# Fourier layer kernel on one Trainium2 core: the inverse row transform of even layers in 32x32 matmul tiles

## The chip, the cores and the metric

The kernel runs on one core of a Trainium2 chip. Time is the device time of one execution in microseconds (us). The kernel before was run 12 times: median 4052.37 us, from 4046.01 to 4058.81 us. One more execution was taken with the hardware profiler, and all views come from that one.

## The reference, cut to what matters

The input x has 8 images of 8 channels, 256 x 256, in float32. Two stages follow each other. The first adds to x a Fourier network of the group-normalised x; the second adds to the result the 3 x 3 maximum (dilation) of its own group-normalised copy.

```python
h = fc0(gn(x) and two coordinate planes)        # 4 groups of 10 channels, 1x1 convolution per group
for i in range(4):                              # the layers, l = 0 .. 3
    xf = rfft2(h); keep 24 row x 12 column frequencies; multiply by complex weights per group
    h1 = irfft2(that)
    h = h1 + conv1x1(h)
    if i < 3: h = swish(h)
h = fc2(swish(fc1(h)))                          # 10 -> 128 -> 2 channels per group
x = x + h
x = x + max3x3(gn(x))
```

The step that changes is the first half of the inverse transform: from the few kept frequencies to all 256 rows.

## The kernel before, in words

**Layout.** One image is held at a time in the tile `h` (128 partitions). The transforms are matmuls with constant tables. A layer `l` of an image `b` runs through these generators, each of which records its instructions and yields now and then:

- `spectrum_h` (or `spectrum_x` for l = 0): forward transform along rows, into the small tile B.
- `mix`: products with the complex weights on the vector engine (L360, L363); the result F is folded by 16 matmuls of 32 x 32 (L379, tile `p_f`) into the tile `fz` (10 channels x 4 groups x 32 frequencies). Each of the four partition quarters q of `p_f` holds three column frequencies; four copies (L395, recorded in the helper as L195 or L193) put them side by side into the first columns of `fz`. For l = 0 a small matmul (L386) and an add (L387) put the mean in.
- `rows_of`: the inverse transform along the rows. For even layers each of the 10 channels is one matmul with a 128 x 128 stationary block of `fz` (4 groups x 32 columns) and the table `rowg` of 264 columns (L405, tile `p_g`). `rowg` holds the same 32 frequencies four times, and the four quarters of `fz` add up in the contraction over 128 partitions. Odd layers use 16 narrower matmuls per channel (L410), with a 32-column output each. Each pair of channels takes one accumulator, which two copies (L195, tile `zt`) empty, and then the generator yields 0.7.
- `layer`: for each of 11 chunks, `burst` adds the inverse column transform (L483) to the 1x1 convolution (L480; L477 for l = 0) in the tile `p_z`; the scalar engine applies the activation (L489, L491).

**Work laid in between.** `head` is the fc1/fc2 part of the image before. It has 128 steps. A step has an fc1 part (L628, four matmuls with 32 rows and 128 output columns, two accumulators, tile `p_fc`; the scalar engine then applies SiLU, L630, once for each accumulator) and, at every second step, an fc2 part (L650, eight matmuls, one accumulator; the vector engine then adds it, L655 or L653). The main loop takes such steps at the yields of the layers, so that the order on the tensor, vector and scalar engines is fixed by the program. `dilate` (tile `m`, L697 to L714) runs in the same way at the yields of the bursts.

**Accumulators.** All of these use one pool in PSUM: `ps_z` hands out four slots in turn, whoever asks. A slot is written again only when what was in it has been read. So the k-th request waits for the readers of request k - 4.

```python
    def ps_z(name):
        return ps.tile([128, 2, 512], F32, tag="z", bufs=4, name=name)
```

Image 0 has no image before it, so its layers run without fc1 and fc2 steps; there the copies alternate between vector and scalar engine (`alone`).

Of the kernel before, what the change touches and what calls it, by code (L numbers as in the profile page):

```python
# [10 lines left out]
F32 = mybir.dt.float32  # L11
AF = mybir.ActivationFunctionType
ALU = mybir.AluOpType
# [5 lines left out]
HW = 256  # L19
NPIX = HW * HW  # L20
G = 4
WID = 10
# [10 lines left out]
NBLK = 3  # L33
NCH = 11
NQ = 4
CS = 2 * NCH
PIX = 2 * HW
DR = 2
# [6 lines left out]
def fno_dilate_kernel(ctx: ExitStack, tc: tile.TileContext, a: dict, out: bass.AP):  # L45
    nc = tc.nc
    mm = nc.tensor.matmul
# [46 lines left out]
    xe = load("xe", (128, 6, G, 5), nc.sync)  # L94
    wext = const.tile([128, G, WID, 5], F32, tag="c_wext", name="c_wext")
    nc.sync.dma_start(wext.rearrange("p g o j -> p (g o j)"), a["wext"].partition_broadcast(128))
    cz = load("cz", (32, 5, WID, G))
    fold = load("fold", (128, 3, 32))
    rowg = load("rowg", (128, NBLK, NQ, CS))
    binv = load("binv", (128, HW))  # L100
    eh_f = load("eh_f", (128, 3, NBLK, 32))
# [70 lines left out]
    for l in range(3):  # L172
# [4 lines left out]
    nc.vector.tensor_tensor(cz[0:1, 0], cz[0:1, 0], cv[0:1], ALU.add)  # L177
    nc.sync.dma_start(cz[25:26, 0], cv[1:2])
    nc.sync.dma_start(cz[0:1, 4], cv[2:3])
    nc.vector.tensor_tensor(  # L180
        wt, wt, io.rearrange("p (l g) -> p l g", l=4).unsqueeze(3).to_broadcast([128, 4, G, 32]), ALU.mult,
    )
# [170 lines left out]
    def mix(b, l, out_):  # L353

        s = [sb.tile([128, 3, G, 2, WID], F32, tag=f"S{i}", bufs=1, name=f"S{i}_{b}_{l}") for i in range(2)]
        bt, sw = out_["bt"], out_["sw"]
        for k in range(3):
            for k2 in range(2):
                pr = turned[:, 2, 1024 * k2 : 1024 * k2 + 800].rearrange("p (g m i) -> p g m i", g=G, i=WID)
                nc.vector.tensor_tensor(  # L360
                    pr, sw[k], bt[:, k2, k].unsqueeze(2).to_broadcast([128, G, 2 * WID, WID]), ALU.mult)
                yield 0.7
                nc.vector.tensor_reduce(  # L363
                    s[k2][:, k].rearrange("p g s o -> p (g s o)"),
                    pr.rearrange("p g m i -> p (g m) i"), AX.X, ALU.add,
                )
                if k == 0 and k2 == 1:
                    sw.append(load_sw(l, 2))
                yield 0.7
        f = sb.tile([128, 2, 3, G, WID], F32, tag="F", bufs=1, name=f"F_{b}_{l}")  # L370
        nc.vector.tensor_tensor(f[:, 0], s[0][:, :, :, 0, :], s[1][:, :, :, 1, :], ALU.subtract)
        nc.vector.tensor_tensor(f[:, 1], s[0][:, :, :, 1, :], s[1][:, :, :, 0, :], ALU.add)
        yield 0.5

        p = ps_a(f"p_f_{b}_{l}")
        for slot in range(2):
            for n, (table, part_of) in enumerate(((0, slot), (1 + slot, 1 - slot))):
                for q in range(4):
                    mm(p[part(q), 120 * slot : 120 * slot + 120], fold[part(q), table, :],  # L379
                       f[part(q), part_of].rearrange("p k g o -> p (k g o)"), start=n == 0, stop=n == 1)  # L380
        nc.vector.tensor_copy(fz[0:32, :, :, 24], cz[:, l])
        if l == 0:
            mr = out_["mr"]
            d = sb.tile([128, 1], F32, tag="d", name=f"dm_{b}")
            nc.vector.tensor_tensor(d, mr[:, 0:1], mr[:, 1:2], ALU.mult)
            mm(p[0:1, 240 : 240 + WID * G], d, wm.rearrange("p o g -> p (o g)"), start=True, stop=True)  # L386
            nc.vector.tensor_tensor(  # L387
                fz[0:1, :, :, 24], fz[0:1, :, :, 24],
                p[0:1, 240 : 240 + WID * G].rearrange("p (o g) -> p o g", o=WID), ALU.add)
        if l < 2:  # L390
            nc.vector.tensor_copy(fz[0:32, :, :, 25], cz[:, 4 if l == 0 else 3])
        for q in range(4):
            dst = fz[part(q), :, :, 6 * q : 6 * q + 6].rearrange("p o g k -> p k g o")
            src = p[part(q), :240].rearrange("p (k g o) -> p k g o", g=G, o=WID)
            copy(q, dst, src)  # L395
        yield 2.5

    def rows_of(b, l):

        zv = zt[:, :, :, : NBLK * WID].rearrange("p r f (n o) -> p o n r f", n=NBLK)  # L400
        for o in range(0, WID, 2):
            p = ps_z(f"p_g_{b}_{l}_{o}")
            for u in range(2):
                if l % 2 == 0:
                    mm(p[:, u, : NBLK * CS * NQ], fz[:, o + u].rearrange("p g k -> p (g k)"),  # L405
                       rowg.rearrange("p n j r -> p (n j r)"), start=True, stop=True)
                else:
                    for g in range(G):
                        for j in range(NQ):
                            mm(p[part(j), u, NBLK * CS * g : NBLK * CS * (g + 1)], fz[:, o + u, g, :],  # L410
                               rowg[:, :, j, :], start=True, stop=True)
            for u in range(2):
                src = p[:, u, : NBLK * CS * NQ]
                if l % 2 == 0:
                    dst = zv[:, o + u].rearrange("p n r f -> p n f r")
                    src = src.rearrange("p (n f r) -> p n f r", n=NBLK, r=CS)
                else:
                    dst = zv[:, o + u].rearrange("p n r f -> p f n r")
                    src = src.rearrange("p (f n r) -> p f n r", f=NQ, n=NBLK)
                copy(u, dst, src)  # L420
            yield 0.7


    def layer(b, l, out_, stored, side):
# [254 lines left out]
    def dilate(b, stats):  # L679
        d = {}  # L680
        yield from stats_end(stats, f"y{b}", d)
        mr = d["mr"]
        whole = y_rows[b % 2][:]
        o_rows = out[b].rearrange("c (p f) -> (c p) f", p=16)
        for r in range(0, 16, DR):
            nc.gpsimd.dma_start(
                yin[:, :, 1 : HW + 1],
                bass.AP(whole.tensor, whole.offset + r * HW, [[16 * HW, 128], [HW, DR + 2], [1, HW]]))
            yield
            yield  # L690

            if r == 0:
                nc.vector.tensor_scalar(yin[:, 0, :], yin[:, 0, :], edge[:, 0:1], None, ALU.min)
            if r == 16 - DR:
                nc.vector.tensor_scalar(yin[:, DR + 1, :], yin[:, DR + 1, :], edge[:, 1:2], None, ALU.min)
            m = sb.tile([128, DR + 2, HW], F32, tag="m", bufs=1, name=f"m_{b}_{r}")
            nc.vector.tensor_tensor(m, yin[:, :, 0:HW], yin[:, :, 1 : HW + 1], ALU.max)  # L697
            yield
            nc.vector.tensor_tensor(m, m, yin[:, :, 2 : HW + 2], ALU.max)
            yield  # L700
            o = sb.tile([128, DR, HW], F32, tag="o", bufs=1, name=f"o_{b}_{r}")
            nc.vector.tensor_tensor(o, m[:, 0:DR], m[:, 1 : DR + 1], ALU.max)
# [12 lines left out]
            yield  # L715
# [73 lines left out]
def _tables():  # L789
# [50 lines left out]
    for j, v in enumerate(planes):  # L840
# [9 lines left out]
    edge[:, 2], edge[:, 3] = np.where(top, PAD, -BIG), np.where(bottom, PAD, -BIG)  # L850
    tables = {
        "fw": fw, "fw8": fw8, "stack": np.tile(np.eye(32), (4, 1)), "eh0": eh0, "eh_f": eh_f.reshape(128, 3, NBLK, 32),
        "rowg": rowg.reshape(128, NBLK, NQ, CS),
        "fold": fold.reshape(128, 3, 32), "binv": binv.reshape(128, HW),
        "xe": xe.reshape(128, 6, G, 5), "grp": grp, "edge": edge,
    }
    return {k: np.ascontiguousarray(v, f32) for k, v in tables.items()}
# [66 lines left out]
```

## Time and profile before

| | |
|---|---|
| median of 12 runs | 4052.37 us |
| profiled execution, its own time | 4050.78 us |
| its span, from the first to the last instruction | 4049.0 us |
| TensorE (PE) busy | 3740.0 us, 92% |
| ScalarE (ACT) busy | 2853.5 us, 70% |
| VectorE (DVE) busy | 2538.3 us, 63% |
| mean granted TensorE clock | 0.976 |
| row matmuls of even layers (L405) | 93.2 us busy, 320 records of 160 matmuls |
| folding matmuls (L379) | 36.7 us busy, 1024 records of 512 matmuls |

A float32 matmul leaves two records in the profile, one for each of its passes. "Busy" is the union of the records of a group, so that matmuls that run at the same time count once. In the chain of waits each stretch of time is put down to the instruction that held up the end.

### The profile page before, as it was taken

The page shows a single profiled execution, that of the slowest core. Times are in us where ns is not written, and L with a number is a line of the kernel's source. Part 1 is how long each engine was busy: PE and PEld are TensorE (multiplying, and loading weights), DVE is VectorE, ACT ScalarE, POOL GpSimd, SP SyncE. Part 2 cuts the span into 40 slices and gives each one's busy share as a digit, 9 for nine tenths or more (in the row PEclk, how much of TensorE's full clock was granted, in tenths as well). Part 3 has the DMA queues.
Part 4 walks back from the last instruction along what each step waited for, and adds up shares of the span by engine and source line. Part 5 has one row for each costly group of instructions (what it writes and reads, how often), then busy time and mean ns, then how long its engine had stood idle before and what let it go on. Part 6 is the DMA issues. An engine that isn't in the chain of part 4 may idle for free.

```text
span 4049.0 us, 118640 instructions
## 1 busy us (share of the span) xinstructions
PE 3740.0 (92%) x53530; PEld 1465.7 (36%) x53530; DVE 2538.3 (63%) x3535; ACT 2853.5 (70%) x2991; POOL 117.3 (3%) x202
## 2 busy tenths in 40 slices
PE   5666999999999999999999999999999999999997
PEld 2333333333333333333333333333333433333222
DVE  6665656556766666765766666666676566673533
ACT  3334777777767777776777777777777777778886
POOL 1000000000000000000000000000000000000000
PEclk8887999999999999999999999999999999999999
DMA  3005111441215321252122611144211532215311
GB/s 84 14 14 187 51 34 42 135 127 57 60 49 176 97 63 58 79 179 63 56 66 89 198 44 52 54 134 151 58 59 49 171 101 64 60 49 192 96 53 46
DMA packets 113986, 345.05 MB, mean 85 GB/s; under 512 B 15769, under 2 KB 18393, under 8 KB 98057
## 3 DMA queue, kind: packets, MB, share of 16 engines
q1 hardware_dynamic: 95288, 276.33, 22.1%
q0 software_dynamic: 18192, 61.13, 4.7%
q8 instruction: 422, 6.91, 0.7%
q14 instruction: 84, 0.68, 0.1%
HBM read 213.40 MB, written 123.74 MB: 83 GB/s over the span
## 4 chain that ended last, share of the span: by engine, by line
PE 78%; DVE 11%; ACT 7%; issue 3%; DMA 1%; POOL 0%; DVEq 0%; POOLq 0%; SPq 0%; ACTq 0%
PE p_fc L650 22%; PE p_fc L628 20%; PE p_z L483 8%; PE p_z L480 7%; PE p_d L448 6%; ACT act L630 4%; PE p_u L462 3%; DVE turned L431 3%; PE p_z L477 2%; PE p_b L333 2%; PE p_g L405 2%; PE p_g L410 2%; ACT h L491 2%; DVE turned L324 2%; DVE turned L201 1%
## 5 line engine op out<-in xcount | busy, mean ns | idle before, releaser
L630 ACT ACTIVATE act<-p_fc 128x1024 f32<-128x1024 f32 x2048 | 1960.2, 1026 | 674.3 <-PE p_fc L628 670.0
L628 PE MATMUL p_fc<-hs,c_w 32*128 32x512 f32 x8192 | 1205.2, 631 | 14.7 <-DVE turned L195 8.5
L650 PE MATMUL p_fc<-act,c_w 128*32 128x512 f32 x8192 | 1001.4, 603 | 47.2 <-ACT act L630 36.0
L628 PEld LDWEIGHTS p_fc<-hs,c_w 32*128 32x128 f32 x8192 | 402.2, 183 | 697.7 <-ACT act L630 278.2
L489 ACT ACTIVATE h<-p_z 128x1024 f32<-128x1024 f32 x528 | 511.8, 1021 | 189.1 <-PE p_z L483 187.7
L431 DVE STREAM_TRANSPOSE turned<-h 128x1024 f32<-128x1024 f32 x528 | 622.9, 1219 | 21.4 <-ACT h L489 21.1
L655 DVE TENSOR_TENSOR y<-p_fc,y 128x512 f32<-128x512 f32 x392 | 270.6, 690 | 498.1 <-PE p_fc L650 496.9
L650 PEld LDWEIGHTS p_fc<-act,c_w 128*32 128x32 f32 x8192 | 227.8, 110 | 649.5 <-issue 348.9
L483 PE MATMUL p_z<-c_binv,zt 32*128 32x256 f32 x5632 | 411.1, 405 | 0.6 <-ACT zt L193 0.6
L480 PE MATMUL p_z<-h,c_wt 32*32 32x512 f32 x8448 | 370.4, 601 | 6.3 <-DVE y L655 2.8
L483 PEld LDWEIGHTS p_z<-c_binv,zt 32*128 32x128 f32 x5632 | 261.4, 186 | 304.5 <-issue 295.0
L448 PE MATMUL p_d<-turned,c_fw 32*32 32x480 f32 (+1 forms) x9216 | 309.5, 539 | 12.5 <-DVE turned L431 12.5
L195 DVE COPY zt<-p_g 128x264 f32<-128x264 f32 x300 | 162.3, 628 | 168.0 <-PE p_g L410 91.4
L491 ACT ACTIVATE h<-p_z,c_bias 128x1024 f32<-128x1024 f32 x176 | 186.6, 1111 | 37.8 <-PE p_z L483 37.5
L199 ACT ACTIVATE turned<-p_d 128x960 f32<-128x960 f32 x144 | 130.2, 904 | 95.5 <-PE p_d L448 95.5
L363 DVE TENSOR_REDUCE S<-turned 128x80 f32<-128x800 f32 x192 | 188.7, 983 | 4.7
L360 DVE TENSOR_TENSOR turned<-t,B 128x800 f32<-128x800 f32 x192 | 188.4, 981 | 1.8 <-DMA t<-in_spw 1.7
L448 PEld LDWEIGHTS p_d<-turned,c_fw 32*32 32x32 f32 x9216 | 121.3, 103 | 187.8 <-issue 150.2
L462 PE MATMUL p_u<-turned,c_stack 128*32 128x480 f32 (+1 forms) x1152 | 137.3, 546 | 42.9 <-DVE turned L201 42.9
L324 DVE STREAM_TRANSPOSE turned<-zt 128x960 f32<-128x960 f32 x96 | 175.5, 1853 | 0.6
L201 DVE COPY turned<-p_d 128x960 f32<-128x960 f32 x144 | 152.1, 1057 | 29.2 <-PE p_d L448 28.9
L480 PEld LDWEIGHTS p_z<-h,c_wt 32*32 32x32 f32 x8448 | 93.6, 103 | 210.6 <-ACT act L630 69.1
(169 smaller groups left out, 1969.5 us busy)
## 6 DMA issues: line engine op xcount, KB each, us to landing
stored<-h SPq DMA_DIRECT2D x88, 1024.0 KB
hs<-stored SPq DMA_DIRECT2D x352, 256.0 KB
t<-in_spw SPq DMA_DIRECT2D x96, 400.0 KB
yin<-y_rows POOLq DMA_DIRECT2D x56, 512.0 KB, 4.9
h<-in_xp SPq DMA_DIRECT2D x352, 48.0 KB
turned<-in_x SPq DMA_DIRECT2D x16, 1024.0 KB
y<-in_x SPq DMA_DIRECT2D x56, 256.0 KB
y_rows<-y POOLq DMA_DIRECT2D x56, 256.0 KB, 2.3
```

The costliest lines, as they stand in the source:

```text
L324: nc.vector.transpose(rows[:, 960 * g : 960 * (g + 1)].rearrange("p (i r) -> p i r", r=32), windows(g))
L431: nc.vector.transpose(dst[:, 2 * i : 2 * i + 2], h[:, c, 2 * i : 2 * i + 2].rearrange("p f (s x) -> p f s x", s=2))
L448: mm(pair[q // 2][part(v % 4), q % 2, : 240 * n], fw8[part(q), v, :], t[part(q), :, :, v, : NBLK * WID], start=v < 4, stop=v >= 4)
L462: mm(p[part(g), : 240 * n], stack, m, start=True, stop=True)
L480: mm(o, wt[part(q), l, g, :], h[part(q), c, f, :], start=True, stop=False)
L483: mm(pair[q // 2][:, q % 2, HW * s : HW * (s + 1)], zt[part(q), 2 * c + s].rearrange("p f o -> p (f o)"), binv[part(q), :], start=False, s ...
L489: nc.scalar.activation(dst, pair[i], AF.Silu)
L491: nc.scalar.activation(dst, pair[i], AF.Identity, bias=bias3)
L628: mm(pair[g // 2][:, g % 2, :], w1[part(g), blk, :], hs[k][part(g), :], start=True, stop=True)
L630: nc.scalar.activation(act[:, 2 * i : 2 * i + 2, :], pair[i], AF.Silu)
L650: mm(acc[part(g), :], w2[:, g, 15 - rb - i : 47 - rb - i], act[:, g, :], start=i == 0, stop=i == 1)
L655: nc.vector.tensor_tensor(y, sums, y, ALU.add)
```

## The change

Even layers: `rowg` is no longer summed over four partition quarters. The fold table is repeated four times along its columns, so that the fold of one quarter q writes its three column frequencies to all four partition quarters; `fz` then holds four full copies of the spectrum. The row matmuls take one copy each: four channels at once, channel u from partition quarter u, with a 32 x 32 stationary tile for each group. Ten matmuls become forty smaller ones, and the blocks are of 4, 4 and 2 channels in place of five pairs. The yields add up to the same 3.5.

The fold needs four accumulators of its own (two requests to the pool, `pair`, in place of one). Odd layers still contract over 128 partitions, and now meet four copies; so the table is divided by 4, and in even layers the copies from `p_f` and the constants `cz` are multiplied by 4. The tile `cz` is spread to four quarters by three DMAs at the start. For l = 0 the mean is put in by four matmuls and four adds. The dilation writes its maximum over `m`, and the tile `o` goes.

```diff
-    fold = load("fold", (128, 3, 32))
+    fold = load("fold", (128, 3, 128))
...
+    for l in (0, 2, 4):
+        nc.vector.tensor_scalar(cz[0:32, l], cz[0:32, l], 4.0, None, ALU.mult)
+    for q in range(1, 4):
+        nc.sync.dma_start(cz[part(q)], cz[0:32])
...
-        p = ps_a(f"p_f_{b}_{l}")
+        pair = [ps_z(f"p_f_{b}_{l}_{i}") for i in range(2)]
+        p = [pair[q // 2][:, q % 2, :] for q in range(4)]
         for slot in range(2):
             for n, (table, part_of) in enumerate(((0, slot), (1 + slot, 1 - slot))):
                 for q in range(4):
-                    mm(p[part(q), 120 * slot : 120 * slot + 120], fold[part(q), table, :],
+                    mm(p[q][:, 120 * slot : 120 * slot + 120], fold[part(q), table, :],
                        f[part(q), part_of].rearrange("p k g o -> p (k g o)"), start=n == 0, stop=n == 1)
...
-            mm(p[0:1, 240 : 240 + WID * G], d, wm.rearrange("p o g -> p (o g)"), start=True, stop=True)
-            nc.vector.tensor_tensor(
-                fz[0:1, :, :, 24], fz[0:1, :, :, 24],
-                p[0:1, 240 : 240 + WID * G].rearrange("p (o g) -> p o g", o=WID), ALU.add)
+            for q in range(4):
+                mm(p[0][32 * q : 32 * q + 1, 240 : 240 + WID * G], d, wm.rearrange("p o g -> p (o g)"),
+                   start=True, stop=True)
+            for q in range(4):
+                row = slice(32 * q, 32 * q + 1)
+                nc.vector.tensor_tensor(
+                    fz[row, :, :, 24], fz[row, :, :, 24],
+                    p[0][row, 240 : 240 + WID * G].rearrange("p (o g) -> p o g", o=WID), ALU.add)
...
         for q in range(4):
-            dst = fz[part(q), :, :, 6 * q : 6 * q + 6].rearrange("p o g k -> p k g o")
-            src = p[part(q), :240].rearrange("p (k g o) -> p k g o", g=G, o=WID)
-            copy(q, dst, src)
+            dst = fz[:, :, :, 6 * q : 6 * q + 6].rearrange("p o g k -> p k g o")
+            src = p[q][:, :240].rearrange("p (k g o) -> p k g o", g=G, o=WID)
+            if alone[0] and q % 2:
+                nc.scalar.activation(dst, src, AF.Identity, scale=factor)
+            else:
+                nc.vector.tensor_scalar(dst, src, factor, None, ALU.mult)
...
-        for o in range(0, WID, 2):
-            p = ps_z(f"p_g_{b}_{l}_{o}")
-            for u in range(2):
-                if l % 2 == 0:
-                    mm(p[:, u, : NBLK * CS * NQ], fz[:, o + u].rearrange("p g k -> p (g k)"),
-                       rowg.rearrange("p n j r -> p (n j r)"), start=True, stop=True)
...
+        rows = rowg.rearrange("p n j r -> p (n j r)")
+        size = 2 if l % 2 else 4
+        for o in range(0, WID, size):
+            n = min(size, WID - o)
+            p = [ps_z(f"p_g_{b}_{l}_{o}_{i}") for i in range((n + 1) // 2)]
+            for u in range(n):
+                for g in range(G):
+                    if l % 2 == 0:
+                        mm(p[u // 2][part(g), u % 2, : NBLK * CS * NQ], fz[part(u), o + u, g, :], rows[part(u)],
+                           start=True, stop=True)
+                        continue
...
-            yield 0.7
+            yield 0.35 * n
...
-            o = sb.tile([128, DR, HW], F32, tag="o", bufs=1, name=f"o_{b}_{r}")
-            nc.vector.tensor_tensor(o, m[:, 0:DR], m[:, 1 : DR + 1], ALU.max)
+            o = m[:, 0:DR]
+            nc.vector.tensor_tensor(o, o, m[:, 1 : DR + 1], ALU.max)
...
-        "rowg": rowg.reshape(128, NBLK, NQ, CS),
-        "fold": fold.reshape(128, 3, 32), "binv": binv.reshape(128, HW),
+        "rowg": rowg.reshape(128, NBLK, NQ, CS) / 4.0,
+        "fold": np.tile(fold.reshape(128, 3, 32), (1, 1, 4)), "binv": binv.reshape(128, HW),
```

More of the change, by code (lines that the diff above doesn't have):

```diff
@@ L96, in fno_dilate_kernel @@
     nc.sync.dma_start(wext.rearrange("p g o j -> p (g o j)"), a["wext"].partition_broadcast(128))
-    cz = load("cz", (32, 5, WID, G))
-    fold = load("fold", (128, 3, 32))
+    cz = const.tile([128, 5, WID, G], F32, tag="c_cz", name="c_cz")
+    nc.gpsimd.dma_start(cz[0:32], a["cz"])
+    fold = load("fold", (128, 3, 128))
     rowg = load("rowg", (128, NBLK, NQ, CS))
@@ L378, in mix @@
                 for q in range(4):
-                    mm(p[part(q), 120 * slot : 120 * slot + 120], fold[part(q), table, :],
+                    mm(p[q][:, 120 * slot : 120 * slot + 120], fold[part(q), table, :],
                        f[part(q), part_of].rearrange("p k g o -> p (k g o)"), start=n == 0, stop=n == 1)
-        nc.vector.tensor_copy(fz[0:32, :, :, 24], cz[:, l])
+        factor = 4.0 if l % 2 == 0 else 1.0
+        nc.vector.tensor_copy(fz[:, :, :, 24], cz[:, l])
         if l == 0:
@@ L384, in mix @@
             d = sb.tile([128, 1], F32, tag="d", name=f"dm_{b}")
-            nc.vector.tensor_tensor(d, mr[:, 0:1], mr[:, 1:2], ALU.mult)
-            mm(p[0:1, 240 : 240 + WID * G], d, wm.rearrange("p o g -> p (o g)"), start=True, stop=True)
-            nc.vector.tensor_tensor(
-                fz[0:1, :, :, 24], fz[0:1, :, :, 24],
-                p[0:1, 240 : 240 + WID * G].rearrange("p (o g) -> p o g", o=WID), ALU.add)
+            nc.vector.scalar_tensor_tensor(d, mr[:, 0:1], factor, mr[:, 1:2], ALU.mult, ALU.mult)
+            for q in range(4):
[6 more added lines that the diff above has]
+                    p[0][row, 240 : 240 + WID * G].rearrange("p (o g) -> p o g", o=WID), ALU.add)
         if l < 2:
-            nc.vector.tensor_copy(fz[0:32, :, :, 25], cz[:, 4 if l == 0 else 3])
+            nc.vector.tensor_copy(fz[:, :, :, 25], cz[:, 4 if l == 0 else 3])
         for q in range(4):
-            dst = fz[part(q), :, :, 6 * q : 6 * q + 6].rearrange("p o g k -> p k g o")
-            src = p[part(q), :240].rearrange("p (k g o) -> p k g o", g=G, o=WID)
-            copy(q, dst, src)
+            dst = fz[:, :, :, 6 * q : 6 * q + 6].rearrange("p o g k -> p k g o")
[4 more added lines that the diff above has]
+                nc.vector.tensor_scalar(dst, src, factor, None, ALU.mult)
         yield 2.5
@@ L400, in rows_of @@
         zv = zt[:, :, :, : NBLK * WID].rearrange("p r f (n o) -> p o n r f", n=NBLK)
-        for o in range(0, WID, 2):
-            p = ps_z(f"p_g_{b}_{l}_{o}")
-            for u in range(2):
-                if l % 2 == 0:
-                    mm(p[:, u, : NBLK * CS * NQ], fz[:, o + u].rearrange("p g k -> p (g k)"),
-                       rowg.rearrange("p n j r -> p (n j r)"), start=True, stop=True)
[L407 to L413, printed above, removed]
+        rows = rowg.rearrange("p n j r -> p (n j r)")
[9 more added lines that the diff above has]
+                        continue
+                    for j in range(NQ):
+                        mm(p[0][part(j), u, NBLK * CS * g : NBLK * CS * (g + 1)], fz[:, o + u, g, :],
+                           rowg[:, :, j, :], start=True, stop=True)
+            for u in range(n):
+                src = p[u // 2][:, u % 2, : NBLK * CS * NQ]
                 if l % 2 == 0:
```

## The prediction

> **What bounds the kernel now.** I read the page first: TensorE is busy 92%, and the chain of waits gives it 78% of the span. The row matmuls that change (L405) hold 2% of that chain, about 81 us; that is the most that can be won. Next I read the chain through one interleaved even layer (image 2, l = 2); columns are start, duration, engine and line, number of records.
>
> ```profile
> 1105.06 1.07 PE p_fc L628 x8
> ...
> 1106.16 1.02 PE p_f L379 x32
> 1107.18 1.25 PE p_fc L628 x8
> 1108.43 1.85 PE p_fc L650 x16
> 1110.29 1.07 PE p_fc L628 x8
> 1111.36 1.09 PE p_g L405 x4
> 1112.45 1.21 PE p_fc L628 x8
> 1113.65 1.09 PE p_g L405 x4
> ...
> 1117.67 1.98 PE p_g L405 x8
> 1119.65 1.23 PE p_fc L628 x8
> 1120.88 1.09 PE p_g L405 x4
> ...
> 1126.06 2.05 PE p_z L480 x32
> ```
>
> The reader is to see that TensorE never rests here and that the five pairs cost 1.09 + 1.09 + 1.98 + 1.09 = 5.25 us. But L628 takes 1.07 us after some neighbours and 1.21 to 1.25 after p_f and p_g: something else is nearly late. The timeline shows what (start, duration, engine, line, operation):
>
> ```profile
> 1104.99 1.14 PE L628 MATMUL p_fc<-hs,c_w 32*128 32x512 f32 x8
> 1106.23 1.94 ACT L630 ACTIVATE act<-p_fc 128x1024 f32<-128x1024 f32 x2 [0.39 <-PE p_fc L628]
> 1107.11 1.32 PE L628 MATMUL p_fc<-hs,c_w 32*128 32x512 f32 x8
> ```
>
> An fc1 part takes 1.07 us of TensorE, but ACT empties its two accumulators only 1.24 us after its start and for 1.94 us more (about 0.97 each). So a slot that the next fc1 must share with this one is free 2.26 us (first) and 3.23 us (second) after the fc1's start, 0.05 for the signal included. At 1107.11 the second half of fc1 needs the first of these and starts 0.19 us late. Four slots go round, and that distance is what the change touches. The chain of an odd layer (image 2, l = 1) shows the same in the fold:
>
> ```profile
> 982.64 1.03 ACT act L630
> 983.67 0.04 issue
> 983.72 1.02 PE p_f L379 x32
> 984.74 1.85 PE p_fc L650 x16
> 986.60 2.50 PE p_fc L628 x16
> ```
>
> Here the fold itself waits for a SiLU of the fc1 two before it. The profiled execution took 4050.78 us (span 4049.0 and 1.8 around it), 1.6 below the median, so my sum starts from 4050.8.
>
> **Row matmuls of even layers.** Removed are 10 matmuls, 5.25 us per layer. Added are blocks of sixteen, sixteen and eight 32x32 matmuls of 264 columns. The nearest row is L480 in the same chain where nothing is late (1007.50, 32 records of 32x32 with 512 columns, 1.11 us): same tiles, same spread over accumulators. One record of 264 columns streams in 0.22 us (records of one L405 pair start 0.22 apart), one of 512 in 0.43. Two passes shorter by 0.21 each give 0.68 us per block; bounds are 0.44 (two passes and nothing else) and 1.11 (L480's own price). Three blocks: 2.0 us. Taken alone, 3.2 us less per layer.
>
> [...]
>
> **Slots of the row blocks.** A block of four channels asks for two slots in a row where a pair asked for one. The order of the built programs on TensorE in l = 2 is: before, fold, fc1, fc2, fc1, pair, fc1, pair, fc2, fc1, two pairs, fc1, pair, fc2, fc1, fc1, burst; after, fold, fc1, fc2, fc1, block, fc1, fc2, fc1, block, fc1, half block, fc2, fc1, fc1, burst. Wherever fc1, block, fc1 stand together, the block takes two of the four slots, and the second fc1 needs exactly both slots of the first. It can't finish its start before 3.23 us after the first one's start, and the next instruction follows 1.07 us after its second half begins (987.97 to 989.03 in the trace). So fc1, block, fc1 costs 4.30 us whether the block takes 0.4 or 1.1; before, fc1, pair, fc1 cost 1.07 + 1.09 + 1.21 = 3.37.
>
> **The fold takes two slots, too.** It moves from one slot to two, in all 32 layers. In even layers fc1, fold, fc1 also becomes 4.30 us, against 3.37 (1104.99 to 1108.36). In odd layers the order is fc1, fc1, fold, fc2, fc1, fc1: the fold's second accumulator is the first fc1's second slot, released one SiLU later (+0.97), with TensorE standing at the fold and fc2 and two fc1 queued behind it.
>
> The fold's own matmuls go from 32 to 128 output columns. Its eight rounds (16 matmuls, two passes, four quarters at once) start 0.10 us apart now. The row for loads of 128 columns one after another is L250: sixteen in 1.73 us, 0.108 each. So eight rounds take 0.87 us, against about 0.95 from start to next start now; no gain or loss that I count. Upper bound: the load's whole duration (L628, 183 ns mean), 1.47 us, +0.6.
>
> **The walk, l = 2** (from the fc1 at 1104.99 as zero). Before: fc2 at 3.37, fc1 at 5.23, and the burst at 21.07, its second half, which waits for the last-but-one fc1's SiLU, at 21.98, the column matmuls at 23.06. After: fc2 at 4.30, +1.86 fc1 at 6.16, block 7.23 to 7.91, fc1's second half at 6.16 + 3.23 = 9.39, fc2 10.46, fc1 12.32, block 13.39, fc1's second half 15.55, half block 16.62 (0.65), fc2 17.27, fc1 19.13, burst's second half at 19.13 + 3.23 = 22.36, column matmuls 23.44. Net +0.4 us: the 3.2 us is spent in three waits. At the block's upper bound +0.8, with a wait less 0 or below: -0.6.
>
> **The walk, l = 0** (six of them, images 2 to 7). The same from the fc1 at 1337.38, with one more price: four adds in place of one (L387, 0.21 each) delay the copies out of the first fold slot until about 4.6, where fc2 wants it at 4.3. Then fc1 6.46, second half 9.69, two fc2 (3.57) from 10.76, fc1 14.33, block, second half 17.56, half block 18.63, fc1 19.26, fc1, burst's second half 22.49 and column matmuls 23.57, against 1360.29 - 1337.38 = 22.91 now. Net +0.65, bounds -0.5 and +1.1.
>
> **The walk, odd layers** (14 of them, images 1 to 7). The second part of the fold starts at 984.66 and not at 983.72; it ends near 985.5, fc2 follows at 985.55 in place of 984.67. The copies out of the fold end 0.9 later and the vector add of fc2 behind them too; the second fc1 needs that add, as now. Net +0.87, bounds 0.6 and 1.5 (slow loads). What follows is TensorE alone up to the burst, so it stays late.
>
> **What is hidden or small.** The copies into `fz` go to 128 partitions, but the width along the partition is the same: an operation on 128 x 40 takes 219 ns (L340) and on 1 x 40 213 (L387). The ten copies out of `p_g` are the same ten (0.63 each). In l = 2 and l = 0 they end before the slots are wanted. The dilation's new maximum over `m` must wait until the output DMA has read `m`; that DMA is issued at 1274.07 and `m` is next written at 1287.64, 13.6 us of cover; a full exposure would be some us for each of 56. At the start three multiplications (0.18 each) and three DMAs on SP stand ahead of seven x-plane loads, which the first burst needs only at 69 us: +0.4. Image 0 has no fc1; there copies set the pace, and smaller blocks start them earlier: about -0.8 for each of its two even layers, +0.6 for the adds. Image 1, l = 0 has no fc1 before its fold: -1.5.
>
> **The sum.** 14 x 0.87 = 12.2; 7 x 0.4 = 2.8; 6 x 0.65 = 3.9; image 1, l = 0 -1.5; image 0 and the start -0.6. Together +16.8: 4050.8 + 16.8 = 4067.6 us. About 0.2% (8 us) is what a measurement of this kernel can tell from no change; this is twice that.
>
> **Rivals.** (1) Faster: the slots don't bind and the row matmuls' 3.2 us arrive on TensorE's chain, 13 x 3.2 + 2.1 = 44 us, 4007 us. For it speaks that the chain is nearly all PE; against it, that both programs' orders make fc1 wait for its predecessor's SiLU. It decides if SiLU's release comes earlier than 2.26 and 3.23 us, below about 1.1 and 2.1. (2) No change: the odd layers pay 12 us, but the even ones come out near their lower bounds (7 x -0.6 + 6 x -0.5 = -7) and with -2.1 the rest is +3, 4054. (3) Slower still: loads of the fold are not hidden (+0.6 in 14 odd layers, 8 us) and blocks cost L480's 1.11 (+0.4 in 13), together 4081.
>
> **How the numbers follow.** My walk 0.62, at 4058 to 4078 (even layers 0.4 us either way, odd ones at 0.7 to 1.0). No change 0.14, faster 0.13, slower still 0.11. Range 4050 to 4080: it leaves out the fast rival and about half of (3). Faster by over 0.2%: 0.13, within 0.14, slower 0.62 + 0.11 = 0.73.
>
> **What would show it.** Right: L405's successor holds about 32 us busy in place of 93; yet fc1 (L628's successor) behind p_f and p_g lasts 2 us in the chain in place of 1.2; ACT takes a larger share of the chain; in odd layers the fold is split by a wait of nearly 1 us. Wrong: fc1 behind a block starting at once, or blocks over 1.2 us, or output DMAs showing up as what `m` waits for.

## The result, and the profile after

The changed kernel takes 4063.65 us (median of 11 runs, 4058.85 to 4068.35); the kernel before, run beside it, 4050.63 us (45 runs, 4040.5 to 4059.42). The ratio is 1.0032, 95% interval 1.0024 to 1.0040: 13 us slower. The profiled execution took 4065.15 us (span 4063.4), 14.4 more than that of before.

The page of the kernel after, its first part and the chain's shares by engine:

```profile
PE 3728.3 (92%) x54538; PEld 1438.7 (35%) x54538; DVE 2528.4 (62%) x3562; ACT 2851.9 (70%) x2991; POOL 117.0 (3%) x202
...
PE 76%; DVE 11%; ACT 8%; issue 4%; DMA 1%; POOL 0%; DVEq 0%; POOLq 0%; SPq 0%; ACTq 0%
```

TensorE works 11.7 us less than before (3740.0), and the whole takes 14 us more: TensorE's share of the chain falls from 78% to 76%, and ScalarE's and "issue" each gain a point. The groups say which work became cheaper and which dearer, first before, then after (line, engine, operation, names, shapes, count, busy us, mean ns, idle time ahead and its releasers):

```profile
L628 PE MATMUL p_fc<-hs,c_w 32*128 32x512 f32 x8192 | 1205.2, 631 | 14.7 <-DVE turned L195 8.5 <-ACT act L630 4.1 <-DVE h L653 1.2
L405 PE MATMUL p_g<-c_rowg,fz 128*128 128x264 f32 x320 | 93.2, 430 | 7.9 <-ACT fz L193 7.9
L379 PE MATMUL p_f<-F,c_fold 32*32 32x120 f32 x1024 | 36.7, 285 | 66.9 <-DVE F L371 47.3 <-issue 15.6 <-ACT act L630 3.9
```

```profile
L647 PE MATMUL p_fc<-hs,c_w 32*128 32x512 f32 x8192 | 1231.5, 633 | 27.7 <-ACT act L649 17.1 <-DVE turned L201 8.5 <-DVE h L672 1.2
L386 PE MATMUL p_f<-F,c_fold 32*128 32x120 f32 x1024 | 48.5, 308 | 72.2 <-DVE F L377 46.6 <-issue 15.6 <-ACT act L649 9.9
L425 PE MATMUL p_g<-c_rowg,fz 32*32 32x264 f32 x1280 | 39.6, 439 | 7.7 <-ACT fz L408 7.4
```

The row matmuls of even layers (L425, L405 before) are busy for 39.6 us in place of 93.2, so the change does what it says (the prediction's sign was about 32); the fold (L386) is busy for 48.5 in place of 36.7, and fc1 (L647), whose matmuls are the same, for 1231.5 in place of 1205.2. The idle time that a SiLU ends ahead of fc1 goes from 4.1 to 17.1 us. Of the 54 us won on the row matmuls the end shows nothing. Where they went is in the chain of waits through the layer that the prediction walked (image 2, l = 2; start, duration, what; `...` stands for rows left out):

```profile
1101.36 1.07 PE p_fc L647 x8
...
1102.46 1.17 PE p_f L386 x32
1103.62 2.02 PE p_fc L647 x8
1105.64 1.85 PE p_fc L669 x16
1107.50 1.14 PE p_fc L647 x8
...
1108.66 1.03 ACT act L649
...
1109.74 2.04 PE p_fc L647 x8
1111.78 1.85 PE p_fc L669 x16
1113.64 1.14 PE p_fc L647 x8
...
1115.88 2.04 PE p_fc L647 x8
1117.92 0.60 PE p_g L425 x16
1118.53 1.85 PE p_fc L669 x16
1120.38 1.14 PE p_fc L647 x8
...
1124.68 1.08 PE p_z L502 x16
```

Two blocks of four channels have vanished from the chain altogether: between the fc1 at 1107.50 and the one at 1109.74 stands ACT's SiLU where the block should be. The fc1 behind a block, and the one behind the fold, last 2.02 to 2.04 us in place of 1.21 to 1.25, because their second half waits for the second SiLU of the fc1 before; behind a block of four channels the first half waits for the first SiLU, too. Only the half block, which takes one slot, is still seen (0.60).

In odd layers the fold itself is cut in two (timeline, image 2, l = 1; the bracket is the idle time and its releaser):

```profile
978.90 0.48 PE L386 MATMUL p_f<-F,c_fold 32*128 32x120 f32 x4 [0.28 <-ACT act L649]
979.81 1.15 PE L386 MATMUL p_f<-F,c_fold 32*128 32x120 f32 x28 [0.43 <-ACT act L649]
```

The first four records go into the first slot (a matmul leaves two records, each with its own weight load: 1024 records and 1024 loads for the 512 matmuls of L386; what the array does in each the traces don't show); the rest start 0.91 us later, when the SiLU of the other slot is done. All 14 folds of odd layers in images 1 to 7 are cut in this way, by 0.91 to 0.92 us.

To see where the time went I took, for every layer of the two profiled executions, the time from the fold's first matmul to the first column matmul (L483, L502). The differences, after less before:

| layers | each, us | sum, us | predicted |
|---|---|---|---|
| odd, images 1 to 7 (14) | 0.19 to 1.52, mean 0.91 | 12.7 | 12.2 |
| l = 2, images 1 to 7 (7) | 0.26 | 1.8 | 2.8 |
| l = 0, images 2 to 7 (6) | 0.85 | 5.1 | 3.9 |
| l = 0, image 1 | 1.13 | 1.1 | -1.5 |
| image 0 (4) | -2.1, -0.2, -3.8, -0.7 | -6.8 | -0.6, start included |

Together 14.0 us; the stretches outside these walks (column matmuls to the next fold, start, end) sum to about nothing, though not each for itself, as told below. The clock is no rival inside the walks of images 1 to 7: apart from image 1, l = 0, none of these 27 walks has a stretch at half clock in either execution.

### The profile page after: what moved, and what is told of

It is laid out like the page before. It is cut to its first block, busy times and chain, and to the rows that moved or that the text cites. A ratio compares the mean times of both kernels' runs of the same rounds, so it can differ in the third digit from the quotient of the medians.

```text
span 4063.4 us, 120753 instructions
## 1 busy us (share of the span) xinstructions
PE 3728.3 (92%) x54538; PEld 1438.7 (35%) x54538; DVE 2528.4 (62%) x3562; ACT 2851.9 (70%) x2991; POOL 117.0 (3%) x202
## 3 DMA queue, kind: packets, MB, share of 16 engines
q1 hardware_dynamic: 95432, 276.41, 21.7%
## 4 chain that ended last, share of the span: by engine, by line
PE 76%; DVE 11%; ACT 8%; issue 4%; DMA 1%; POOL 0%; DVEq 0%; POOLq 0%; SPq 0%; ACTq 0%
PE p_fc L669 22%; PE p_fc L647 20%; PE p_z L502 8%; PE p_z L499 7%; PE p_d L467 6%; ACT act L649 5%; PE p_u L481 3%; PE p_z L496 2%; DVE turned L450 2%; PE p_b L339 2%; PE p_g L429 2%; ACT h L510 2%; DVE turned L330 1%; DVE turned L207 1%; PE p_f L386 1%
## 5 line engine op out<-in xcount | busy, mean ns | idle before, releaser
L649 ACT ACTIVATE act<-p_fc 128x1024 f32<-128x1024 f32 x2048 | 1960.1, 1026 | 689.1 <-PE p_fc L647 685.0
L647 PE MATMUL p_fc<-hs,c_w 32*128 32x512 f32 x8192 | 1231.5, 633 | 27.7 <-ACT act L649 17.1
L647 PEld LDWEIGHTS p_fc<-hs,c_w 32*128 32x128 f32 x8192 | 407.8, 184 | 735.8 <-ACT act L649 340.2
L502 PE MATMUL p_z<-c_binv,zt 32*128 32x256 f32 x5632 | 410.8, 405 | 0.7 <-ACT zt L199 0.7
L502 PEld LDWEIGHTS p_z<-c_binv,zt 32*128 32x128 f32 x5632 | 261.1, 186 | 306.4 <-issue 296.0
```

Source lines behind the costliest of these rows:

```text
L502: mm(pair[q // 2][:, q % 2, HW * s : HW * (s + 1)], zt[part(q), 2 * c + s].rearrange("p f o -> p (f o)"), binv[part(q), :], start=False, s ...
L647: mm(pair[g // 2][:, g % 2, :], w1[part(g), blk, :], hs[k][part(g), :], start=True, stop=True)
L649: nc.scalar.activation(act[:, 2 * i : 2 * i + 2, :], pair[i], AF.Silu)
```

## The experiments

The diffs below show the lines that matter, against the changed kernel (for the SiLU pair, against the kernel before and the changed one); `...` marks what is left out.

My theory: the pool's four slots, handed out in turn, let an fc1 write only after its predecessor's SiLU when fold or block take two slots between them. Rivals: the new matmuls are slow in themselves; or the loss lies elsewhere (copies, adds, the clock). The runs fall into three sets, each with runs of before beside it: its medians were 4049.48 us (20 runs; the first four experiments), 4050.00 (17; the SiLU pair, the odd layers' fold in all images, image 0 in wide matmuls) and 4050.61 (21; the odd layers' fold in images 1 to 7, the last version). "Fold to column" is the walk of the table above.

**The fold alone.** The new fold and four copies stay, the row matmuls are those of before.

```diff
+                if l % 2 == 0:
+                    mm(p[0][:, u, : NBLK * CS * NQ], fz[:, o + u].rearrange("p g k -> p (g k)"), rows,
+                       start=True, stop=True)
+                    continue
...
-        size = 2 if l % 2 else 4
+        size = 2
...
-        factor = 4.0 if l % 2 == 0 else 1.0
+        factor = 1.0
```

> The fold of the change alone (two slots, 128 columns, four copies of the spectrum), with the row matmuls of even layers as before (ten of 128x128, five pairs). Theory (the slots: the fold's second slot makes the next fc1 or the fold itself wait for a SiLU): odd layers +0.9 us each (14), even ones +1.0 (13), about +25 us against the kernel before, 4076. Rival A (the small row blocks cost the time, the fold nothing): within 5 us of the kernel before. Rival B (the 128-column loads of the fold are slow): slower too, but by the fold's own length, with no wait on a SiLU inside it.

Measured: 4079.10 us, ratio 1.0070 (1.0055 to 1.0084), +29.6. Fold to column: l = 2 +0.92 each, l = 0 +1.50, odd layers +12.1 in all. So all of the loss, and more, comes with the fold and what goes with it (wide copies, adds, the dilation's edit, which this run keeps); the row blocks give back about 16 us of it (29.6 - 13), and not the 54 that they save on TensorE.

**Blocks of two channels, one slot each**, fold as changed.

```diff
-        size = 2 if l % 2 else 4
+        size = 2
```

> The change with row blocks of two channels (one slot each, five blocks) in place of four. Theory: a block of two takes 0.63 us where the pair took 1.09, but its neighbours still share slots with the SiLU; the fold costs what it cost: +12.5 in odd layers, about +0.1 in even ones, image 0 about -5, so +5 to +14 us, like the change itself. Rival A (small blocks are slow): five blocks cost more than three, +20 us or more.

Measured: 4062.55 us, ratio 1.0030 (1.0020 to 1.0039), +13.1, at the upper end of what I expected. Locally the even layers are a little better (l = 2 -0.05 each, l = 0 +0.54), the odd ones little changed (+10.7 in all). With the fold in two slots the blocks' size hardly matters.

**The fold in one slot.** Two copies of the spectrum: 64 columns, two quarters side by side in one slot.

```diff
-        pair = [ps_z(f"p_f_{b}_{l}_{i}") for i in range(2)]
-        p = [pair[q // 2][:, q % 2, :] for q in range(4)]
+        pt = ps_z(f"p_f_{b}_{l}")
+        p = [pt[64 * (q % 2) : 64 * (q % 2) + 64, q // 2, :] for q in range(4)]
...
-            dst = fz[:, :, :, 6 * q : 6 * q + 6].rearrange("p o g k -> p k g o")
+            dst = fz[0:64, :, :, 6 * q : 6 * q + 6].rearrange("p o g k -> p k g o")
...
-        size = 2 if l % 2 else 4
+        size = 2
```

> Two copies of the spectrum in place of four: the fold has 64 columns, two quarters lie side by side in one bank, so that it takes one slot as before; row blocks of two channels in 32x32 tiles, one slot each. No request to the pool differs from the kernel before. Theory: odd layers 0, even layers -0.9 each (13), image 0 about -4: -16 us, 4035 (from 4050.6). Rival A (small blocks slow): no gain, or slower. Rival B (slow loads of the fold, half as many columns): +5 or more from the odd layers.

Measured: 4046.00 us, ratio 0.9991 (0.9981 to 1.0001), -3.5 in place of -16: by the whole time a miss. By the walks it is nearer: l = 2 -0.97 each, l = 0 -0.61 each, odd layers +0.8 in all, so -9.6 where the slots decide. What was lost lies in images 0 and 1, at whose end the profiled run (4051.76, 5.8 above the median) stood 7.3 us behind before. In the stretch of 0 to 450 us of before and of this kernel (busy times of PE, PEld, DVE, ACT and POOL, then granted clock, DMA share, GB/s) TensorE is busy for as long, VectorE and ScalarE for 5 and 7 us less, as in a kernel that is 7 us behind; the clock is lower:

```profile
0.00:450.00 450.00, 296.71 (x5762) 156.69 (x5762) 285.28 (x401) 185.29 (x208) 11.29 (x26) 0.85 0.23 71
```

```profile
0.00:450.00 450.00, 297.28 (x5774) 149.90 (x5776) 280.19 (x400) 178.21 (x201) 11.30 (x26) 0.81 0.22 71
```

In the clock's records it is 1.0 or 0.5, nothing between; 0.85 is 133 us at half, 0.81 is 174 us. (Over the 20 runs of before, a mean clock lower by 0.001 goes with 2.8 us more; carried over to this kernel, whose runs have 0.9724 in the mean where before has 0.9762, that would be 11 of the missing us. It is a correlation, not an experiment.) The run with image 0 in wide matmuls takes this up.

**Blocks of four with the fold in one slot**, each fold quarter copied twice to make four copies of the spectrum.

```diff
+            for half in range(2):
+                dst = fz[64 * half : 64 * half + 64, :, :, 6 * q : 6 * q + 6].rearrange("p o g k -> p k g o")
...
-        pair = [ps_z(f"p_f_{b}_{l}_{i}") for i in range(2)]
+        pt = ps_z(f"p_f_{b}_{l}")
```

> Row blocks of four channels as in the change, but the fold in one slot (64 columns, two quarters side by side), and eight copies out of it so that there are four copies of the spectrum. Theory: odd layers 0 (unless eight copies of 0.6 us delay the vector add of fc2), l = 2 about -0.6, l = 0 about 0, image 0 about -5: -5 to -10 us; a block of four still makes the next fc1 wait for its predecessor's SiLU, so it gains less than blocks of two (e3). Rival (the block's slots do not matter): more than e3, -20 us or more.

Measured: 4133.72 us, ratio 1.0210 (1.0188 to 1.0231), +84: a clear miss. Its group of fc1 on TensorE:

```profile
L648 PE MATMUL p_fc<-hs,c_w 32*128 32x512 f32 x8192 | 1255.3, 640 | 66.1 <-DVE fz L411 44.5
```

A new wait, for `fz`: eight copies follow the fold (timeline, image 2, l = 1), and the slot is free only after the last:

```profile
1000.51 1.05 PE L386 MATMUL p_f<-F,c_fold 32*64 32x120 f32 x32 [0.28 <-ACT act L650]
1001.63 4.70 DVE L411 TENSOR_SCALAR fz<-p_f 64x240 f32<-64x240 f32 x8 [0.99 <-PE p_f L386]
1006.48 2.71 PE L648 MATMUL p_fc<-hs,c_w 32*128 32x512 f32 x8 [1.99 <-DVE fz L411]
```

I had counted the copies as hidden. They hold the one slot for 5.8 us after the fold's start, which is longer than any SiLU does (3.23). The walks show where that costs: odd layers +49.7 in all, l = 0 in images 2 to 7 +17.8, l = 2 but +2.4. And with the waits goes more time at half clock: after 450 us this kernel has some 116 us at half clock, before 63; one such stretch follows the wait shown, from 1006.98, and the fc1 in it lasts 2.71 us. How the 84 us divide between wait and clock I did not isolate.

**SiLU at half length, before and after.** ACT's release was the disputed quantity, so I shortened it in both kernels. Only the first half of the columns goes through SiLU; the rest of `act`, now four fixed tiles used in turn, is held at zero.

```diff
-            act = sb.tile([128, G, 512], F32, tag="act", bufs=4, name=f"act_{b}_{n}")
+            act = act_tiles[n % 4]
...
-                nc.scalar.activation(act[:, 2 * i : 2 * i + 2, :], pair[i], AF.Silu)
+                nc.scalar.activation(act[:, 2 * i : 2 * i + 2, :256], pair[i][:, :, :256], AF.Silu)
```

> The kernel before, with the SiLU of fc1 taken over the first 256 of the 512 columns of every accumulator only (the other half of act is held at zero), so that ACT needs about 0.55 us an accumulator in place of 0.97. The slot theory: the release of an fc1's two slots moves from 2.26 and 3.23 us after its start to about 1.8 and 2.35. In before nothing of size waited for them in the even layers; odd layers lose the 1 us for which the fold waits for a SiLU, so this kernel is some 10 to 40 us faster than before (the closing part of each burst waits for a SiLU, too). Its use is as the base of the next run.

> The changed kernel with the same SiLU over the first 256 of the 512 columns. The slot theory: fc1, block, fc1 now costs 2.35 + 1.07 = 3.4 us in place of 4.3, and the row blocks' own saving comes through. Walked with 0.55 us per SiLU, changed less unchanged is -1.6 us in each of seven l = 2, -0.8 in each of six l = 0, +0.2 in each of 14 odd layers: about -13 us against the run before with the same SiLU, and some -7 more in image 0, so the sign turns from +13 to -13 or below. The rival that the 32x32 blocks or the loads of the wide fold are slow in themselves: the difference stays at +13.

Measured: before with it 3982.06 us, ratio to before 0.9839 (0.9826 to 0.9852); after with it 3958.88, ratio to before 0.9781 (0.9769 to 0.9794). The sign turns: the change costs 13 us with the full SiLU and brings 23 with the half (expected 13 and some 7 more). Fold to column, after less before: l = 2 six times -1.77 and once -1.50 (expected -1.6), l = 0 -0.48 each (expected -0.8), odd layers -3.4 in all, where I expected +0.2 each, so a gain and not the small loss. The chain of the changed kernel with the short SiLU, image 2, l = 2:

```profile
1093.54 1.14 PE p_fc L647 x8
...
1094.71 0.61 ACT act_tile L649
1095.32 0.04 issue
1095.36 1.61 PE p_fc L647 x6
1096.97 1.85 PE p_fc L669 x16
```

From the fc1 ahead of the block to the fc2 behind the next fc1 are 3.43 us; with the full SiLU 4.28 (1107.50 to 1111.78). The same matmuls, the same blocks, the same copies: what differs is the SiLU (598 ns in the mean for 128 x 512, 1026 for 128 x 1024). The rival that tiles or loads are slow in themselves falls. One number missed: the unchanged kernel gained 68 us in place of my 10 to 40, of which only 19.5 lie in the walks from fold to column. I had looked at these walks alone, and the SiLU ends waits outside them, too (before, image 2, l = 1: the fc2 at 979.55 starts 0.04 us after the end of a SiLU, ahead of the fold at 983.72).

**The odd layers' fold as before.** Changed kernel, but odd layers fold 32 columns into one slot; their row matmuls contract over 32 partitions, with the factor 4 in the copies.

```diff
+        if l % 2:
+            p = ps_a(f"p_f_{b}_{l}")
...
+                        mm(p[part(q), 120 * slot : 120 * slot + 120], fold[part(q), table, :32],
...
-                        mm(p[0][part(j), u, NBLK * CS * g : NBLK * CS * (g + 1)], fz[:, o + u, g, :],
-                           rowg[:, :, j, :], start=True, stop=True)
+                        mm(p[0][part(j), u, NBLK * CS * g : NBLK * CS * (g + 1)], fz[0:32, o + u, g, :],
+                           rowg[0:32, :, j, :], start=True, stop=True)
```

> The changed kernel, but in odd layers the fold gives 32 columns into one slot as before (its copies go to 32 partitions, and the odd row matmuls contract over these 32 alone, with the factor 4 in the copies). Even layers are as changed. The slot theory: the 12.7 us that the 14 odd layers lost come back and the time is 4050.6 + 13 - 12.7, so 4051 +- 3. The rival that the odd layers lose by something else than the fold's second slot (the wide copies, what the even layers leave late): it stays at +13, 4063.

Measured: 4060.76 us, ratio 1.0033 (1.0021 to 1.0044), +10.8: nearly the rival's number. In the walks the odd layers lose 1.7 us in all in place of 12.7, just as the theory says; but by the end of image 1 this run stood 6.7 us behind before, the changed kernel 0.9 ahead of it. From there to the last column matmuls it lost 4.6 us, the changed kernel 14.3. Image 0 was altered too, and had more time at half clock (181 us of the first 450, the changed kernel 157). So I ran it again with images 1 to 7 alone altered:

```diff
-        if l % 2:
+        if b > 0 and l % 2:
```

> The run with the odd fold as before lost no more than 1.7 us in the odd layers of images 1 to 7 (12.7 in the changed kernel), yet its total moved only from +13 to +11: up to the end of image 1 it stood 7.6 us behind the changed kernel, in layers whose fold and row matmuls it had also altered in image 0, where no fc1 is, and with 181 us at half clock in the first 450 us (157 in the changed kernel). Here image 0 is wholly that of the changed kernel, and only the odd layers of images 1 to 7 fold into one slot. If the odd layers' loss is the second slot: 4063.65 - 11 = 4052.7, +-3. If something outside those walks gives it back whatever image 0 does: 4060 or more.

Measured: 4056.45 us (12 runs, 4045.59 to 4060.68), ratio 1.0015 (1.0007 to 1.0024), +5.8. That is 7.2 below the changed kernel, with odd layers at +3.4 in place of +12.7. It falls 0.8 us short of the range that I gave (4049.7 to 4055.7), and 3.6 below the rival's 4060. Part of the missing is the clock again. One l = 2 walk in this run (image 7) lost 1.91 us where the other six lost 0.26. The row of that walk and of a piece of it:

```profile
3521.50:3545.40 23.90, 22.61 (x253) 7.00 (x252) 9.82 (x20) 14.77 (x16) 0.54 (x1) 0.93 0.21 63
3537.80:3541.20 3.40, 3.40 (x20) 0.72 (x16) 1.17 (x3) 0.32 (x1) 0.00 (x0) 0.50 0.36 121
```

For 3.4 us the clock is at 0.50 with TensorE busy all the time, and the walk is 1.65 us longer than its six fellows, about half of that.

**Image 0 in wide row matmuls, the rest in one slot.** To learn whether the small blocks of image 0 cost the clock:

```diff
+        wide = b == 0 and l % 2 == 0
+        factor = 2.0 if l % 2 == 0 and not wide else 1.0
...
+                if b == 0 and l % 2 == 0:
+                    mm(p[0][:, u, : NBLK * CS * NQ], fz[:, o + u].rearrange("p g k -> p (g k)"), rows,
+                       start=True, stop=True)
+                    continue
```

> The version with the fold in one slot and blocks of two channels, but with image 0's two even layers in 128x128 row matmuls (over 64 partitions, factor 1). In the version without that, images 2 to 7 gain about 8 us, l = 2 of image 1 one more, yet the time moved by only -3.5 us, and the granted clock was half for 174 us of the first 450 where before had 133. If the small blocks in image 0 cost the clock there, this kernel has about 133 us at half clock and takes 4036 to 4042; if the clock of the first 450 us has another cause, it has about 170 us and stays near 4046.

Measured: 4044.37 us, ratio 0.9988 (0.9979 to 0.9997), and 147 us at half clock in the first 450: between the two expectations. The form of image 0's rows seems to have a part in it. Over the profiled executions with 128x128 rows in image 0 I count 126 to 147 us at half clock there, over those with 32x32 blocks 150 to 181. With one profile of each kernel that is a pattern, not a proof.

**A version that beats both.** Image 0 as in the changed kernel (it has no fc1 to share slots with), images 1 to 7 with the fold in one slot and blocks of two channels.

```diff
+        w = 64 if b > 0 else 128
+        if b > 0:
+            pt = ps_z(f"p_f_{b}_{l}")
+            p = [pt[64 * (q % 2) : 64 * (q % 2) + 64, q // 2, :] for q in range(4)]
+        else:
+            pair = [ps_z(f"p_f_{b}_{l}_{i}") for i in range(2)]
+            p = [pair[q // 2][:, q % 2, :] for q in range(4)]
...
-        size = 2 if l % 2 else 4
+        size = 2 if l % 2 or b > 0 else 4
```

> Image 0 as in the changed kernel (fold in two slots, four copies, blocks of four channels), images 1 to 7 with the fold in one slot, two copies of the spectrum and blocks of two channels. From the runs so far, against before: l = 2 seven times -0.96, l = 0 six times -0.6, odd layers 0, together -10.3, and image 0 and 1 -1 to -2 as in the changed kernel: 4038 to 4041. If the half clock in images 0 and 1 rises as with blocks of two in image 0 (174 us of the first 450 in place of 157), it stays near 4046.

Measured: 4040.06 us (9 runs, 4036.07 to 4043.53), ratio 0.9975 (0.9965 to 0.9985): 10.5 us faster than before, as expected in the sum. The terms were not all so: l = 2 and l = 0 gave -6.8 and -3.6, but the odd layers lost 4.1 where I had nothing, and by the end of image 1 the run stood 4.6 ahead, more than I had counted. Its chain through the same layer:

```profile
1098.48 1.05 PE p_f L391 x32
1099.53 1.22 PE p_fc L654 x8
1100.76 1.85 PE p_fc L676 x16
1102.61 1.07 PE p_fc L654 x8
1103.68 0.60 PE p_g L432 x16
1104.29 1.69 PE p_fc L654 x8
```

The fc1 behind the fold is back at 1.22 us, and the first block stands in the chain with its own 0.60. The fc1 behind that block still takes 1.69, so that fc1, block, fc1 come to 3.36 us where fc1, pair, fc1 were 3.37 before: even here what this block saves goes into the same wait.

## Why the prediction was right

I forecast 4067.6 us (range 4050 to 4080) and slower with 0.73; measured 4063.65. The sum was made from a profiled execution; that of the changed kernel took 4065.15.

- **The release times** (2.26 and 3.23 us after the fc1's start) carry the whole case, and held. Predicted for l = 2, counted from the fc1 at 1101.36: fc2 at 4.30, fc1 at 6.16, fc2 at 10.46, fc1 at 12.32, half block 16.62, fc1 19.13, column matmuls 23.44. Measured: 4.28, 6.14, 10.42, 12.28, 16.56, 19.02, 23.32. In the timeline the two halves of the fc1 behind the first block start 2.31 and 3.22 us after the fc1 before it (1107.43 to 1109.74 and 1110.65). The half-SiLU pair shows by experiment that it is ACT's release, and not the row matmuls, that sets these steps.
- **The odd layers** (12.2) measured 12.7, each fold cut by a wait of 0.91 us. With the fold back in one slot 1.7 and 3.4 are left in the walks. This step is shown for the sum. The single layers scatter from 0.19 to 1.52, four of 14 below the lower bound of 0.6; that the sum agrees to half a microsecond is in part luck. And behind the fold the walk isn't quite as forecast: in image 2, l = 1 the two fc1 that were to wait for the fc2 add as before last 2.01 us in place of 2.57 (timeline, 982.75 and 986.53), and the row matmuls after them wait 0.30 us for a SiLU. What sets the single layers stays open.
- **l = 2** (0.4 each) measured 0.26: the steps drift early to 0.12 us, 0.05 of it at the half block (0.60 in the chain, not 0.65).
- **l = 0** (0.65) measured 0.85. Why it is 0.2 more I did not isolate; that the four adds delay the copies further than I counted is a guess.
- **The block's own time**, 0.68 us by the two passes, is 0.77 in the timeline (32 records at 1108.50). It decides nothing, as claimed: the block isn't in the chain. The fold's loads are hidden: first to last record 0.90 us in even layers against 0.76, so 0.14, where the upper bound had 0.6. This part of the rival "slower still" is out, and so is its other part, a block at 1.11.
- **Image 1, l = 0, and image 0** are the terms that failed in the walks. I gave -1.5 and -0.6; the walks show +1.1 and -6.8. Neither was worked out from rows. In the even layers of image 0 the changed kernel gains 2.1 and 3.8 us, where I had 0.8 each; with the wide row matmuls kept (the fold alone) these two walks gain 0.0 and 1.1, so most of it comes with the smaller blocks. In image 1, l = 0 the two walks can't be compared as they stand: 18.0 us of it ran at half clock after, 7.7 before. But between the walks of image 0 and that of image 1, l = 0 3.6 us were lost again, so that the total up to the column matmuls of image 1, l = 0 stood at -2.1, where I had -2.1: a right sum of wrong terms. The clock of that stretch (157 us at half in the first 450, before 133) is a likely part of the loss, not an isolated one.
- **The later clock**, which I left out altogether, went the other way: after 450 us the changed kernel's profile has 46 us at half clock, that of before 63 (some 22 of either at the very end), and the stretches between the walks of images 2 to 7 sum to -4 us; so these images cost 14.3 us, where their walks lost 18.3.
- **The dilation's edit** was costed at nothing because `m` is written 13.6 us after its output DMA is issued. The maximum's idle time ahead of it, for which that DMA could have shown, is still put down to the input's DMA (24.2 of 24.7 us; 22.6 of 23.0 before): no new wait.
- **What decides** is the emptying of accumulators and not the row matmuls: these are busy 2.4 times less (39.6 us in place of 93.2), and the whole is 13 us slower. The traces show whose emptying it is: that of fc1 (1.94 us of ACT for its two), a neighbour which the change doesn't touch.
- **Two readings ahead of the sum** were rough. The 81 us that the row matmuls could give came from a share rounded to 2%; it is 2.2%, 89 us. And TensorE does rest once in the stretch whose chain is shown: 0.24 us for a SiLU ahead of the burst at 1126.06. Neither enters the sum.

The fast rival needed ACT to release below about 1.1 and 2.1 us. The half SiLU comes to about 1.8 and 2.4 (1093.54 to 1095.36, and 3.43 less 1.07), and already turns the sign; so the rival's mechanism is real, and I put its point too low: part of the gain comes through well before all of it does.

## What to carry to other kernels

When several producers draw on one pool of accumulators in turn, count the slots that each request takes before counting its matmuls: a second slot asked for between two others shortens the time which an earlier reader has to finish, and a saving on TensorE can then turn into a wait of the same size (here 54 us off the row matmuls, and 13 us more in all). Walk the order of the built program with the release times of the trace; it gave every step of an l = 2 layer to 0.12 us here, l = 0 to 0.2, and the odd layers only in the mean. Keep the copies out of a shared slot few: the version with eight of them in the fold's slot was 84 us slower than before, the one with four 3.5 faster (they differ in the size of the row blocks, too; the idle time ahead of fc1 that the copies end is 44.5 us).

## What the runs showed of the hardware

The granted TensorE clock goes with effects of the size under study. Its half-rate stretches come in multiples of 3.413 us in the records (3.413, 6.827, 10.24, ...; 21 stretches before, 18 after), apart from the last one of a run (21.7 and 22.1 us), and one of them cost 1.65 us where TensorE was the bound (the walk shown; a second one of 3.4 us at 0.50, with TensorE busy all the time, stands in an l = 2 walk of image 6 in the run with the odd layers' fold as before in all images). They differ between executions (the mean clock of the 20 runs of before goes from 0.974 to 0.978) and between kernels, mostly in the first 450 us, where TensorE is busy for only 297 of them in the kernel before: 126 to 181 us of the 450 were at half clock. What brings such a stretch these runs don't show: in the 3.41 us ahead of each one after 450 us, the last apart, TensorE was busy for 0.97 to 3.41 us before (nine stretches) and 0.97 to 3.27 after (seven; 0.97 ahead of the one at 1189.73). Why the blocks of image 0 should bring more of them stays open. Of the 3.8 us between what the odd layers' experiment was to give back (11) and what it gave (7.2), 1.7 stand in the odd layers' own walks (3.4 lost, where 1.7 had been counted on) and 1.65 in the one stretch shown; what is left is less than these medians can tell.
